# Two samples traced in the order of a table instead of turn by turn, in a four-layer attention kernel

## The chip, the core and the metric

The kernel runs on one core of one Trainium2 chip. The metric is device time of one execution in microseconds (us). TensorE is called PE here, VectorE DVE, ScalarE ACT, GpSimd POOL and SyncE SP, as in the profile.

## What is computed

The input is 16 samples of 256 channels by 32 x 32 positions, fp32. Four layers follow each other, each sample by itself:

```python
# layer 0 and layer 2 (own weights):
h = group_norm(x, 8 groups); q, k, v = linear(h)
x = x + proj(softmax(q.T @ k / 16) @ v)
# layer 1, a gate over positions:
m, M = mean(x, channels), max(x, channels)
x = x * sigmoid(conv3x3(m + M + relu(conv3x3([m, M]))))
# layer 3, q and k of 32 channels:
e = clip(q.T @ k / sqrt(32), -10, 10)
x = gamma * (softmax(e) @ v) + x
```

## The kernel before, in words

**Stages of a sample.** Layers 0 and 2 (`attend`) fold the query and key weights into one 256 x 256 matrix. First `seven` makes t = m x (banks tb, ta, tc, tf), then the values (`values`, banks vb, va, vc, vf). Then for each half h of the positions come two groups of logits (`logits`, banks sb, sa, sc, sf), their exponentials on ACT (L988, L990), and the product with the values (`weighted`, banks b, af, c). All these block products take seven block multiplications in place of eight, with sums and differences of blocks made on DVE. All go through one helper, so that their matmuls have one line, L877. A product's result is copied from its PSUM bank by ACT (L978 for logits, L1047 to L1063 in `weighted`) or added by DVE (L909, L1031). `weighted` makes combinations of the exponentials on DVE (L1004, L1005, L1050, L1056), and ends with the scaled residual (L1036).

**The gate.** `gate_of` makes two short matmul groups (c1 at L473, and c2). c1 reads row tiles that DVE and ACT shift by one position (`neighbours`, L458 and L459).

**Layer 3.** `clipped_attend` makes q and k with matmuls of 64 columns (`qk_products`, copied at L1394 and by ACT), values by `values`, and scores in sets. A set (`score_products`, L1401) is one h and one half mh of the keys: four tiles of 32 rows side by side on PE, each in a bank of its own, two matmuls a tile. ACT takes the exponentials from the four banks (`exponentials`, L1417), DVE clips them (`clip`, L1426), and `weighted` follows. A sample has four sets, 64 in all.

**Banks.** All products take banks from one PSUM pool of eight, in traced order: a new tile gets a bank that its previous tile's last reader has left.

**Lanes and turns.** Sample b runs on lane b % 2; even samples are `stream(0)`, odd ones `stream(1)`, both Python generators. A third, `later()`, holds the strips of layer 0's bias (L699), the head of sample 1, the weight transposes and folds of layers 2 and 3 (L623, L635), the gate's tables and checks of the weights. Each `yield` ends a turn; a turn issues a few products and what belongs to them. `wait(n)` spends n turns on nothing, for instance two between two score sets (`W_EXP`). The main loop (L1770 to L1776) gives `stream(0)` 30 turns ahead, each with one of `later`, and then goes turn by turn.

**Who orders what.** Only PE keeps the traced order. For DVE, ACT, POOL and SP, `Plan` makes the order after tracing: `durations` prices each step, `run` places step after step, `room` and `ready` tell when a step's tiles can have space, `needed` ranks steps by when PE wants them, and `pin` repeats that `ROUNDS` times, keeps the best and fixes each engine's order by dependences without a semaphore.

**Loads.** Inputs are issued on SP at the start (L554 x, L574 the layer-2 weights). The first tb_l waits for the normed x of sample 0 (L446).

Of the kernel before, what the change touches and what calls it, by code (L numbers as in the profile page):

```python
# [17 lines left out]
C = 256  # L18
# [20 lines left out]
L0_GAMMA, L0_BETA, L0_BQ, L0_BK, L0_BP = range(5)  # L39
L2_GAMMA, L2_BETA, L2_BQ, L2_BK, L2_BP = range(5, 10)  # L40
NVEC = 10
OFFSET = 30
ROUNDS = 3


W_PLANES, W_GATE1, W_GATE2, W_SEND1, W_NORM1, W_NORM2, W_NORM3, W_SEND2, W_EXP, W_AV, W_AV3 = 9, 2, 2, 4, 2, 10, 4, 7, 2, 2, 0
# [17 lines left out]
)  # L64
PE, DVE, ACT, POOL, SP = range(5)
SEEN = 44, 23, 23, 100, 60
RESTART, ENTRY, MARGIN = 102, 93, 1.04


class Book:  # L70
# [32 lines left out]
def elements(ap):  # L103
    return math.prod(n for _, n in ap[1:])


def durations(engine, ins, outs, reads, mode):


    ap = outs[0].ap  # L110
    n, parts = elements(ap), ap[0][1]
    if engine == PE:
        n = elements(reads[0].ap)
        if ins.is_transpose:
            return 110, 287
        if mode:
            return {"rows": (135, 496), "columns": (253, 403), "corner": (121, 210)}[mode]
        return max(224, 1.66 * n + 8), max(287, 0.84 * n + 178)
    if ins.opcode == "DMACopy":
        if "DRAM" in str(outs[0].tensor.space):  # L120
            return 480, 2500
        if n == 1024:
            return 480, 4600
        return 600, 5600 if n == 512 else 7200
    if engine == POOL:
        return 460 + 2 * n, 640 + 2 * n
    psum = any("PSUM" in str(a.tensor.space) for a in outs + reads)
    partial = 100 * (parts < P)
    if engine == ACT:
        issue = 50 + 0.83 * n if psum else 80 + 0.86 * n  # L130
        issue = MARGIN * max(210, issue + 100 * (len(reads) > 1) + partial)
        issue += 200 * (len(outs) - 1)
        return issue, issue + 180
    n = max([n] + [elements(a.ap) for a in reads])
    if ins.opcode not in ("TensorScalarPtr", "TensorCopy", "Reciprocal") or psum:
        issue = 60 + 1.045 * n
    elif sum(elements(a.ap) == n for a in reads) > 1:
        issue = 60 + 1.28 * n
    else:
        issue = 70 + 0.51 * n + 60 * max(0, len(reads) - 1)  # L140
    issue = MARGIN * max(90, issue + partial)
    return issue, issue + 157


class Plan:
# [79 lines left out]
    def run(self, rank):  # L225


        steps, n = self.steps, len(self.steps)
        begin, end = [0.0] * n, [None] * n
        free, mode = [0.0] * 5, ""  # L230
        live, next_of, placed = {}, dict.fromkeys(self.queues, 0), set()
        products = [i for i in range(n) if steps[i].engine == PE]
        at, missing = 0, [len(s.behind) for s in steps]
        waiting = [[i for i in range(n) if steps[i].engine == e and not missing[i]] for e in range(5)]
        order = [[] for _ in range(5)]

        def last_use(name):
            last = 0.0
            for j in self.users[name]:
                if end[j] is None:  # L240
                    return None
                last = max(last, end[j])
            return last

        def room(name):

            of, bufs = self.book.tiles[name]
            held = live.setdefault(of, [])
            if self.queues[of][next_of[of]] != name:
                return None  # L250
            if len(held) < bufs:
                return 0.0, None
            return min(
                ((t, o) for o in held for t in [last_use(o)] if t is not None), default=None
            )

        def ready(i):
            s = steps[i]
            t = 0.0
            for j in s.behind:  # L260
                if not steps[j].engine == s.engine == PE:
                    t = max(t, end[j])
            for name in s.tiles:
                if name not in placed:
                    r = room(name)
                    if r is None:
                        return None
                    t = max(t, r[0])
            return t and t + SEEN[s.engine]

        def place(i, t):
            nonlocal mode
            s = steps[i]
            for name in s.tiles:
                if name in placed:
                    continue
                placed.add(name)
                of, _ = self.book.tiles[name]
                old = room(name)[1]
                if old is not None:  # L280
                    live[of].remove(old)
                live[of].append(name)
                next_of[of] += 1
            more = 0
            if s.engine == PE:
                more = RESTART * (t > free[PE] > 0)
                if s.mode != mode:
                    t, more = (t + ENTRY, more) if s.mode else (t, RESTART)
                mode = s.mode
            begin[i], end[i] = t, t + s.done + more  # L290
            free[s.engine] = t + s.issue + more
            order[s.engine].append(i)
            for j in s.ahead:
                missing[j] -= 1
                if not missing[j] and steps[j].engine != PE:
                    waiting[steps[j].engine].append(j)

        for _ in range(n):
            best = None
            if at < len(products) and not missing[products[at]]:  # L300
                r = ready(products[at])
                if r is not None:
                    best = max(free[PE], r), products[at]
            for e in (DVE, ACT, POOL, SP):
                times = [(max(free[e], r), i) for i in waiting[e] for r in [ready(i)] if r is not None]
                if times:
                    t = min(times)[0]
                    i = min((rank[i], i) for u, i in times if u <= t + 1)[1]
                    if best is None or t < best[0]:
                        best = t, i  # L310
            t, i = best
            if steps[i].engine == PE:
                at += 1
            else:
                waiting[steps[i].engine].remove(i)
            place(i, t)
        return free[PE], order, begin
# [19 lines left out]
    def pin(self, tc):  # L337


        best, rank = None, [(0.0, i) for i in range(len(self.steps))]  # L340
        for _ in range(ROUNDS):
            found = self.run(rank)
# [167 lines left out]
def fast_path(nc, tc, k, bad, x, w_l0, w_l2, w_l3, qk_bias, v_bias, tap_idx, out):  # L510
# [7 lines left out]
    with ExitStack() as ctx:  # L518
# [328 lines left out]
        rows = [wts.tile([P, 3, STRIP], FP, name=f"rows{lane}") for lane in range(2)]  # L847
# [145 lines left out]
        def weighted(e, vt, tv, y, ri, h, nm):  # L993
# [30 lines left out]
            n0, n1 = h * TPH, h * TPH + 2  # L1024

            c1, c2 = slice(0, P), slice(P, C)
            lo, hi = slice(0, 2), slice(2, 4)
            acc = combp.tile([P, TPH, C + 1], FP, tag="acc", name=f"acc_{nm}_{h}")
# [29 lines left out]
            c = bank(f"c_{nm}_{h}")[:, : 2 * (P + 1)].rearrange("p (i c) -> p i c", i=2)  # L1058
            go(s1, t1, c, lone=False)
            nc.scalar.copy(acc[:, hi, P:], c)  # L1060
            yield
            go(s2, t2, b, fresh=False)
            nc.scalar.copy(acc[:, lo, c2], b)  # L1063
# [4 lines left out]
            for i in range(2):  # L1068
                done(i)
            yield  # L1070
            nc.vector.reciprocal(ri[:, n1 : n1 + 2], acc[:, hi, C])
            go(s3, t3, b, fresh=False)
            plus(hi, c2, b)
            plus(hi, c1, b)
# [644 lines left out]
        ready, tokens, late, running = {}, {}, [], [0]  # L1719
# [3 lines left out]
        def do_chores(lane, n=None):  # L1723
            for do in chores[lane][:n]:
                do()
            del chores[lane][:n]
# [3 lines left out]
        def in_turn(gens):  # L1730

            gens = list(gens)
            while gens:
                for g in list(gens):
                    if next(g, gens) is gens:
                        gens.remove(g)
                    else:
                        yield

        def later():  # L1740

            in_strips(bcol0, bstrip0, "l0")
            chores[0].extend(to_tokens(tokens[0]))
            yield from in_turn([head(1), fold("l2", 1, L2_GAMMA)])
            yield from fold3()
            chores[1].extend(to_tokens(tokens[1]))
            yield from k.build_toep(tc, work, tidx)
            yield from checks()

        def stream(first):  # L1750
            for b in range(first, B, 2):
                if b > 1:
                    chores[first].extend(to_tokens(tokens[b]))
                for _ in sample(b):
                    do_chores(first, 1)
                    yield
            do_chores(first)
            if first in running:
                running.remove(first)
# [7 lines left out]

        streams = [stream(0), stream(1)]  # L1770
        rest = later()
        for _ in range(OFFSET):
            next(streams[0])
            next(rest, None)
        for _ in in_turn([in_turn(streams), rest]):
            pass  # L1776


# [319 lines left out]
```

## Time and profile before

| what | us |
|---|---|
| median of 3 runs | 2646.5 (2644.03 to 2647.04) |
| the profiled execution, whole | 2642.92 |
| its span in the profile | 2641.1 |
| PE busy | 2622.2 |
| DVE busy | 2143.3 |
| ACT busy | 1349.1 |

The granted clock is 0.999 on average. An engine's busy time is the union of its instructions' time; the difference of the span to PE's busy time is not all of what PE waits, because a matmul's record also lasts through a short stall. For that the starts of single records are needed. In a timeline, the columns are start, duration, engine, line, operation, output and inputs with their sizes, number of records, and in brackets the idle time before and what ended it. A matmul on full fp32 data has two records.

### The profile page before, as it was taken

The numbers are of one execution on the slowest core, as the hardware profiler recorded it, in microseconds if no ns is written. First come the engines' busy times: TensorE is split into PE (matmuls) and PEld (weight loads), VectorE is DVE, ScalarE is ACT, GpSimd is POOL, SyncE is SP. The second block draws the span as 40 slices with busy tenths as digits, with TensorE's granted clock in tenths as the row PEclk, the third lists the DMA queues.
The fourth block names the chain that finished last, engine by engine and source line by source line (L and its number), as shares of the span: only waits on it lengthen the run. The fifth ranks groups of instructions, "written<-read, shape, count | busy, mean of one in ns | idle before, by whom it ended". The sixth has DMA issues, their size and how long they took to land.

```text
span 2641.1 us, 47888 instructions
## 1 busy us (share of the span) xinstructions
PE 2622.2 (99%) x18998; PEld 2368.0 (90%) x18998; DVE 2143.3 (81%) x4180; ACT 1349.1 (51%) x2825; POOL 69.7 (3%) x172
## 2 busy tenths in 40 slices
PE   8999999999999999999999999999999999999998
PEld 7888899888988989989889898998989989899897
DVE  8798887988778887788877888778887788878776
ACT  5454455544565445554555545555455544545453
POOL 5000000000000000000000000000000000000000
PEclk9999999999999999999999999999999999999999
DMA  4021211112121120211201212112111121101111
GB/s 118 1 65 49 57 33 37 53 49 65 25 57 49 41 73 9 57 56 41 65 17 49 65 33 65 32 34 65 49 49 33 33 65 49 49 17 33 49 39 44
DMA packets 135878, 123.08 MB, mean 47 GB/s; under 512 B 12768, under 2 KB 126688, under 8 KB 135648
## 3 DMA queue, kind: packets, MB, share of 16 engines
q1 hardware_dynamic: 133776, 118.76, 16.4%
q8 instruction: 153, 2.51, 0.4%
q10 hardware_dynamic: 1872, 1.18, 0.1%
q14 instruction: 77, 0.63, 0.1%
HBM read 69.58 MB, written 50.33 MB: 45 GB/s over the span
## 4 chain that ended last, share of the span: by engine, by line
PE 98%; DVE 1%; ACT 0%; DMA 0%; issue 0%; SPq 0%; DVEq 0%; ACTq 0%
PE b_l L877 19%; PE af_l L877 13%; PE c_l L877 13%; PE sb_l L877 13%; PE sc_l L877 8%; PE vb_l L877 5%; PE sf_l L877 4%; PE sa_l L877 4%; PE vc_l L877 3%; PE tb_l L877 3%; PE s L1401 3%; PE tc_l L877 2%; PE vf_l L877 2%; PE va_l L877 1%; PE tf_l L877 1%; PE qk L1375 1%
## 5 line engine op out<-in xcount | busy, mean ns | idle before, releaser
L877 PE MATMUL sb_l<-t_l,x 128*128 128x256 f32 x1024 | 256.9, 381 | 0.0
L877 PE MATMUL b_l<-vt,e_l 128*128 128x128 f32 x2048 | 250.2, 275 | 0.0
L877 PEld LDWEIGHTS b_l<-vt,e_l 128*128 128x128 f32 x2048 | 242.6, 192 | 4.9 <-issue 2.3
L988 ACT ACTIVATE e_l<-e_l 128x512 f32<-128x512 f32 x256 | 160.4, 630 | 119.0 <-DVE e_l L909 118.4
L877 PEld LDWEIGHTS sb_l<-t_l,x 128*128 128x128 f32 x1024 | 185.0, 190 | 31.8 <-issue 10.3
L978 ACT COPY e_l<-sb_l 128x512 f32<-128x512 f32 x256 | 149.1, 583 | 103.9 <-PE sb_l L877 102.3
L909 DVE TENSOR_TENSOR e_l<-sc_l,e_l 128x512 f32<-128x512 f32 x128 | 88.2, 689 | 119.2 <-PE sc_l L877 94.2
L877 PE MATMUL c_l<-tv,cb_l 128*128 128x129 f32 x1504 | 184.0, 275 | 0.0
L1417 ACT ACTIVATE e<-s 128x512 f32<-128x512 f32 x256 | 133.8, 601 | 97.0 <-PE s L1401 96.1
L909 DVE TENSOR_TENSOR e_l<-sb_l,e_l 128x512 f32<-128x512 f32 x256 | 172.9, 683 | 9.6 <-PE sb_l L877 5.0
L877 PEld LDWEIGHTS c_l<-tv,cb_l 128*128 128x128 f32 x1504 | 176.7, 191 | 0.8
L990 ACT ACTIVATE e_l<-e_l 128x1024 f32<-128x1024 f32 x128 | 135.2, 1056 | 76.2 <-DVE e_l L909 76.0
L793 ACT ACTIVATE xr<-xr,bstrip 128x128 f32<-128x128 f32 (+1 forms) x376 | 141.5, 437 | 16.2 <-DMA xr<-in_x_dram 10.2
L877 PE MATMUL sf_l<-tc_l,x 128*128 128x256 f32 x512 | 132.4, 381 | 0.0
L877 PE MATMUL sc_l<-tc_l,xs_l 128*128 128x256 f32 x512 | 131.6, 379 | 0.0
L877 PE MATMUL sa_l<-t_l,x 128*128 128x256 f32 x512 | 131.4, 379 | 0.0
L877 PE MATMUL sc_l<-t_l,xs_l 128*128 128x256 f32 x512 | 131.4, 379 | 0.0
L877 PE MATMUL sb_l<-tc_l,xs_l 128*128 128x256 f32 x512 | 131.4, 379 | 0.0
L877 PE MATMUL af_l<-vt,e_l 128*128 128x128 f32 x1024 | 127.2, 277 | 0.0
L877 PEld LDWEIGHTS af_l<-vt,e_l 128*128 128x128 f32 x1024 | 119.4, 192 | 8.1 <-issue 8.1
L877 PE MATMUL b_l<-tv,e_l 128*128 128x128 f32 x1024 | 125.7, 275 | 0.0
L877 PE MATMUL c_l<-vt,e_l 128*128 128x129 f32 x1024 | 125.4, 275 | 0.0
(304 smaller groups left out, 5840.6 us busy)
## 6 DMA issues: line engine op xcount, KB each, us to landing
x<-mid_x SPq DMA_DIRECT2D x64, 512.0 KB, 3.6
xr<-in_x_dram SPq DMA_DIRECT2D x64, 256.0 KB, 5.0
mid_x<-t_z SPq DMA_DIRECT2D x128, 128.0 KB, 2.3
mid_x<-t_l SPq DMA_DIRECT2D x128, 128.0 KB, 2.3
x<-in_x_dram SPq DMA_DIRECT2D x62, 256.0 KB, 3.8
out_dram<-xr SPq DMA_DIRECT2D x124, 128.0 KB, 2.3
raw_l<-in_w_l_dram SPq DMA_DIRECT2D x1, 1024.0 KB, 6.8
raw_l<-in_w_l_dram SPq DMA_DIRECT2D x2, 256.0 KB, 4.3
```

The lines of the kernel that those rows point to most:

```text
L793: nc.scalar.activation(y[:, s, ts], y[:, s, ts], AF.Identity, bias=bias[:, s : s + 1])
L877: mm = nc.tensor.matmul(out, left, right, start=fresh and m == 0 and (lone or i == 0), stop=(m == len(pairs) - 1), skip_group_check=True,)
L909: nc.vector.tensor_tensor(dst, src, dst, ALU.add)
L978: nc.scalar.copy(block(i, j), ps.rearrange("p (m n) -> p m n", m=2))
L988: nc.scalar.activation(part, part, AF.Exp)
L990: nc.scalar.activation(e[:, m : m + 2, :], e[:, m : m + 2, :], AF.Exp)
L1375: nc.tensor.matmul(ps[i * PH : (i + 1) * PH, : qt * P].rearrange("p (g n) -> p g n", g=qt), w3qk[:, c, i], xt[:, g0 : g0 + qt, c], start=( ...
L1401: nc.tensor.matmul(ss[g][:, j * 2 * P : (j + 1) * 2 * P].rearrange("p (t g j) -> p t g j", t=TPH, g=2), qk[gs, mh, 1 - blk, j * P : (j + 1 ...
L1417: nc.scalar.activation(by_strip[:, :, :, qa], ss[g].rearrange("p (m t n) -> p m t n", m=2, t=TPH), AF.Exp,)
```

## The change

Four parts. The numbers of lines in the new file are 36 higher from `weighted` on.

1. The tables FIRST_TURNS, TURNS (used CYCLES = 4 times) and LAST_TURNS name for each turn whose it is: 0 and 1 are the two streams, 2 is `later`. What the tables leave over goes turn by turn.
2. `ready` lets a tile be reserved only by its first traced use.
3. `Plan`'s constants change, among them the prices of the row and column tiles and of entering and leaving them, and a rule is added: an engine is held for a step of higher rank that becomes ready before the chosen one would end, and is needed within AHEAD.
4. In `weighted`, one reciprocal moves two turns ahead, directly behind ACT's copy that it reads.

```diff
-OFFSET = 30
-ROUNDS = 3
+FIRST_TURNS = (
+    "22222000000220000000000202000000020022022200200222002200010000221112100010100011"
...
+TURNS = (
+    "00000010111100111111100011001111111000110111111111011000100111000111111000111100"
...
+LAST_TURNS = (
+    "00000010111100111111100011001111111000110111111111011000100111000111111000111100"
...
+CYCLES = 4
+ROUNDS = 4
-RESTART, ENTRY, MARGIN = 102, 93, 1.04
+RESTART, ENTRY, EXIT, MARGIN = 102, 190, 205, 1.04
+AHEAD = 1000
-            return {"rows": (135, 496), "columns": (253, 403), "corner": (121, 210)}[mode]
+            return {"rows": (108, 496), "columns": (216, 403), "corner": (121, 210)}[mode]
-                    if r is None:
+                    if r is None or self.users[name][0] != i:
                         return None
-                    t, more = (t + ENTRY, more) if s.mode else (t, RESTART)
+                    t, more = (t + ENTRY, more) if s.mode else (t, EXIT)
                     i = min((rank[i], i) for u, i in times if u <= t + 1)[1]
+                    late = t + steps[i].issue
+                    soon = [
+                        (rank[j], u, j)
+                        for u, j in times
+                        if t + 1 < u < late and rank[j] < rank[i] and 1 < rank[j][0] < late + AHEAD
+                    ]
+                    if soon:
+                        _, t, i = min(soon)
             nc.scalar.copy(acc[:, hi, P:], c)
+            nc.vector.reciprocal(ri[:, n1 : n1 + 2], acc[:, hi, C])
             yield
...
-            nc.vector.reciprocal(ri[:, n1 : n1 + 2], acc[:, hi, C])
             go(s3, t3, b, fresh=False)
-        streams = [stream(0), stream(1)]
-        rest = later()
-        for _ in range(OFFSET):
-            next(streams[0])
-            next(rest, None)
-        for _ in in_turn([in_turn(streams), rest]):
+        streams = [stream(0), stream(1), later()]
+        for turn_of in FIRST_TURNS + CYCLES * TURNS + LAST_TURNS:
+            next(streams[int(turn_of)], None)
+        for _ in in_turn(streams):
             pass
```

More of the change, by code (lines that the diff above doesn't have):

```diff
@@ L41 @@
 NVEC = 10
-OFFSET = 30
-ROUNDS = 3
+FIRST_TURNS = (
+    "22222000000220000000000202000000020022022200200222002200010000221112100010100011"
+    "01121020220101002111112112200220011111221211111222201102220221012111100102121122"
+    "22000111102001000000001010000000010000010111101111111001000100100000000001000101"
+    "10011101001101111110011010111110111111100001010101110001111110101010000010000111"
+    "11111111000001000001000001110110110100000000000110110101001000101011111000000010"
+    "00101101011000010001000011111001111111000110011111111101111111110110001001110001"
+    "11111000111100001000011100000100000101101010111110001101000100000000001011100111"
+    "01011011111001001100101111101111111000100000110001101000010111000000111110011111"
+    "10111111000010010000111111100100110000110101100010111111000000001000001011001000"
+    "0110000101"
+)
+TURNS = (
+    "00000010111100111111100011001111111000110111111111011000100111000111111000111100"
+    "00100001110000010000010110101011111000110100010000000000101110011101011011111001"
+    "00110010111110111111100010000011000110100001011100000011111001111110111111000010"
+    "0100001111111001001100001101011000101111110000000010000010110010000110000101"
+)
+LAST_TURNS = (
+    "00000010111100111111100011001111111000110111111111011000100111000111111000111100"
+    "00100001110000010000010110101011111000110100010000000000101110011101011011111001"
+    "00110010111110111111100010000011000110100001011100000011111001111110111111000010"
+    "01000011111110010011000011010110010111110101000011110000001100001010000101111000"
+    "01111111000110011111000001100100100111100001111101101011111010111001111001000011"
+    "10000010000001000101000010000001011111000110100000111011001100010101101111100100"
+    "11001011111011111110001110111000011110000000011111000101101110111110100010010011"
+)
+CYCLES = 4
+ROUNDS = 4
 W_PLANES, W_GATE1, W_GATE2, W_SEND1, W_NORM1, W_NORM2, W_NORM3, W_SEND2, W_EXP, W_AV, W_AV3 = 9, 2, 2, 4, 2, 10, 4, 7, 2, 2, 0
```

## The prediction, as put on record

> **What bounds the kernel now.** I read the page first: the busy shares, then the chain that ended last.
>
> ```profile
> span 2641.1 us, 47888 instructions
> ...
> PE 2622.2 (99%) x18998; PEld 2368.0 (90%) x18998; DVE 2143.3 (81%) x4180; ACT 1349.1 (51%) x2825; POOL 69.7 (3%) x172
> ...
> PE 98%; DVE 1%; ACT 0%; DMA 0%; issue 0%; SPq 0%; DVEq 0%; ACTq 0%
> ```
>
> TensorE (PE) is busy 99% of the span and is 98% of the chain. So the time is PE's matmuls plus whatever gaps stand between them. The change orders the same matmuls differently (the built programs hold the same PE instructions), so only gaps can move. Next, the list of PE's waits:
>
> ```profile
> PE wtp_l L623 <- DMA raw_l<-in_w_l_dram: 4.8, 1, 4.8
> PE tb_l L877 <- DVE x L446: 2.0, 1, 2.0
> PE s L1401 <- DVE t_qk L1394: 1.7, 2, 0.9
> PE fold_l L635 <- DVE wt_l L629: 1.0, 1, 1.0
> ```
>
> About 10 us are named, all in the first 46 us or the last 50. The steady state hides its gaps in "busy", so I went to single records. Two back-to-back matmul records of 128 columns start 112 ns apart, of 256 columns 216 ns apart. Over a whole cycle (two samples, 324.3 us), only two kinds of place exceed that. The first is a score visit, that is, PE going into the 32-row tiles of layer 3 and back out. The timeline of PE shows it:
>
> ```profile
> 1012.65 1.03 PE L877 MATMUL sb_l<-t_l,x 128*128 128x256 f32 x4
> 1013.51 1.95 PE L877 MATMUL b_l<-vt,e 128*128 128x128 f32 x16
> 1015.39 1.15 PE L1401 MATMUL s<-t_qk 32*128 32x256 f32 x16
> 1016.47 2.05 PE L877 MATMUL b_l<-vt,e_l 128*128 128x128 f32 x16
> 1018.36 1.95 PE L877 MATMUL af_l<-tv,e_l 128*128 128x128 f32 x16
> ```
>
> Read start to start. Undisturbed, 16 records of a block product take 16 x 0.112 = 1.79. Here b_l lasts 1.88 before s and 1.89 after it, and s takes 1.08 where four rounds of four tiles side by side, at 0.216 a round, would be 0.865. The excess is 0.09 + 0.10 + 0.215 = 0.41 us a visit. The 64-column visits of q and k are untouched by the change.
>
> The second kind is the gate's first matmul (c1, L473) of the odd lane, which waits for ACT:
>
> ```profile
> 163.79 0.83 PE L877 MATMUL va_l<-wvp_l,x 128*128 128x128 f32 x6
> ...
> 164.38 0.24 ACT L459 COPY rows<-rows 32x62 f32<-32x62 f32 x1
> 164.67 0.52 PEld L473 LDWEIGHTS c_l<-rows,toep 128*128 128x128 f32 x4 [0.24 <-ACT rows L459]
> 164.67 0.63 PE L473 MATMUL c_l<-rows,toep 128*128 128x32 f32 x4
> ```
>
> ACT ends at 164.62, c1 starts at 164.67, 323 ns after the record before it instead of 112; the next record follows after 133 instead of 31. That is 0.31 us, the same in all eight cycles.
>
> **The change, part by part.**
>
> *Fewer score visits.* Comparing the built orders, before makes 64 score visits of one set; after makes 47: 30 of one set and 17 of two sets back to back. A second set appended costs its 4 x 0.216, and no entry or exit. Gain: 17 x 0.41 = 6.9 us. The Trainium skill (TensorEngine Tiling (Array Packing), Key Properties) says that changing the tiling mode drains the engine; that gives the sign, the row gives the price.
>
> *What the pairs cost.* The same page speaks against pairing: Gotcha 1, PSUM Pressure, says different row tiles write to different banks and software must synchronise them. Two sets take eight banks, all that the pool has. Taken at its harshest (the second set cannot start before the other users' banks are drained and the pair pays a full drain), the page would have the pair lose what it gained; so I walked it. In all 17 pairs but the last, the built order gives the fourth tile of the second set the bank of b_l of the sample's layer-3 (or of the other lane's layer-2) product, which closes just before the visit. It is freed by the two adds L1031 acc<-b. Taking DVE's prices from the rows below, for the odd-lane place (b, c, b of layer 3 after the last sb of layer 0; S is the end of sb):
>
> ```profile
> 1012.85 0.17 DVE L1066 RECIPROCAL ri<-c_l 128x2 f32<-128x2 f32 x1 [1.02 <-PE c_l L877]
> 1012.94 0.41 DVE L1031 TENSOR_TENSOR acc_l<-c_l,acc_l 128x256 f32<-128x256 f32 x1
> 1013.72 0.69 DVE L909 TENSOR_TENSOR e_l<-sb_l,e_l 128x512 f32<-128x512 f32 x1 [0.37 <-PE sb_l L877]
> ...
> 1015.32 1.21 DVE L1004 TENSOR_TENSOR cb_l<-e_l 128x1024 f32<-128x1024 f32 x1
> ```
>
> DVE starts 0.20 after the PE group that it waits for has given way (c_l to sb_l at 1012.65, reciprocal at 1012.85). So: first sb add S+0.21 to 0.90; ACT's exponential (L988, 0.63) to S+1.6; L1004 from S+1.65, L1005 from S+2.8, both 1.14 apart, free at S+3.95; reciprocal and acc<-c to S+4.35; two L1036 at 0.39 to S+5.15. b_l closes at S+3x1.79 = S+5.37, the adds run from S+5.57 to S+6.32 (0.34 spacing, 0.41 the second), seen by PE about 0.05 later (as c1 after ACT): S+6.37. The visit starts at S+5.37+0.09; the second set's fourth tile is due 0.32 + 3 x 0.216 + 0.02 after that: S+6.45. So it is just in time, by 0.08. In the even lane b_l follows sb directly, the adds have nothing ahead of them, and the margin comes out the same. Weights for a round are loaded one round ahead in the records (at S+6.23), so the load is late although the matmul need not be; c1 shows that an unhidden load costs about 0.1. Bounds: 0 (it hides) and 0.1 plus any DVE slip, say 0.3. I take 0.05, nearer to the walk: 17 x 0.05 = 0.8 us. Below nothing is excluded, since a wait is added and none taken away here.
>
> *Behind a pair* stand the first ACT exponential (L1417; starts 1.16 after the visit's start, as 1016.55 against 1015.39, 0.49 apart, 0.60 long) and the bank it frees: free at 1.8 from the visit's start, next full product due at 1.94. The copies L978 of the next logits stand after three exponentials in ACT's order, not after eight. DVE's clips (L1426) are due over 5 us later. I cost these at nothing; the cover is those 0.1 us and, further back, the logits or block products of the other lane.
>
> *c1 of the odd lane* now stands behind vb of layer 2, some 4.5 us of PE later; ACT's copy keeps its time. Gain 8 x 0.31 = 2.5 us. What reads c1 has 9.6 us of PE work as cover before c2 instead of 12.3, for a chain of 4 to 5 us.
>
> *Front.* The layer-2 weight transposes (L623) and the strips (L699) now stand ahead of the first tb_l (L877), which waited for DVE until 16.08. Their data is issued on SP at 10.08 and the page has that load landing after 6.8, so 16.9:
>
> ```profile
> 10.08 0.62 SPq L574 DMA_DIRECT2D raw_l<-in_w_l_dram  x1
> ```
>
> PE's idle of 2.0 (14.05 to 16.08) becomes 14.05 to 15.4 and 15.8 to 16.9, together 2.4: +0.4 us. The granted clock is 0.50 from 15.78 to 19.20 and 1.00 beside it. The Trainium skill (TensorE: Matmul & The Clock Gate, Part 1) ties half clock to an idle window of about 3.4 us; were another window lost by that rule, it would cost up to 1.7. Range -1 to +2.1; I take the idle sum. SP's and POOL's own orders do not change in the built programs.
>
> *No price:* the reciprocal two turns earlier (0.12 to 0.17 of DVE, not on the path), the planner's new constants and its rule of holding an engine (nothing on the chip), and runs of one lane's logits instead of alternating ones: such runs stand in before too, without a wait.
>
> **The sum.** 2642.9 (the profiled execution; span 2641.1 and 1.8 around it) - 6.9 - 2.5 + 0.8 + 0.4 = 2634.7, which is 8.2 less. Against the median of the runs, 2646.5, that is 2638.3. 0.2% (5.3 us) is about what a measurement of this kernel can tell from no change.
>
> **The rivals.**
> A (0.55): as summed, 2638.3; it runs from 2635.5 (pairs free, front gains 1) to 2641.
> B (0.20): the fourth bank is late by some tenths. For it: the margin is 0.08 and DVE is 81% busy. At 0.3 us a pair, 5.1 of the 9.0 net gain are lost: 2646.5 - 6.9 - 2.5 + 0.4 + 5.1 = 2642.6.
> C (0.14), slower: the full eight banks. After a pair the next logits need a bank from the exponentials, and their second product needs ACT's copy L978; if that copy waits behind all eight exponentials (1.16 + 8 x 0.49, then the copy's 0.58: 5.7 after the start, due at 4.5), each pair loses over 1.1 us. The break-even is 9.0/17 = 0.53 us a pair, slower by 0.2% from 0.84. At 1.0: 2646.5 - 9.0 + 17 = 2654.5. Against it: the copy stands after three exponentials.
> D (0.11): the gains come, but the new DVE and ACT orders put a wait of about 1 us into each cycle elsewhere: about 2646. For it: every product waits on one of those engines; against it: the covers that I found exceed 1 us.
>
> Faster: A and a little of B, 0.57. Within 0.2%: most of B and of D, 0.28. Slower: C and some of D, 0.15. The range runs from 2635 to 2648.5, leaving out most of C.
>
> **What would show it.** Right: 47 visits in the timeline, with score groups of 32 records of about 1.95 us; no c_l L473 wait on ACT in mid-run; PE busy less by about 9 us. B or C: a new line "s L1401 <- DVE acc" among PE's waits, or "sb_l <- ACT", and a two-set visit longer than 1.95. The front: first tb_l near 18 instead of 16.08. I am wrong if the 0.41 of a visit is not saved when two sets join, or if PE's sum falls and DVE's or ACT's idle before a product rises as much.

## The result and the profile after

The changed kernel takes 2637.66 us (median of 7 runs, 2635.85 to 2638.16) against 2645.96 for the kernel before (7 runs, 2642.59 to 2647.04): ratio 0.9969, 95% interval 0.9958 to 0.9981, so 8.3 us less. Measured once more on another occasion, the ratio was 0.9969 again (0.9958 to 0.998). The profiled executions differ by less: 2635.5 against 2641.1 of span, 5.6 us, and the same two kernels profiled a second time gave 2635.2 and 2641.1. I return to that difference below.

The page of the changed kernel, the same three rows:

```profile
span 2635.5 us, 48049 instructions
...
PE 2617.8 (99%) x18998; PEld 2374.0 (90%) x18998; DVE 2156.0 (82%) x4180; ACT 1348.8 (51%) x2825; POOL 74.2 (3%) x172
...
PE 98%; DMA 1%; ACT 0%; DVE 0%; SPq 0%; issue 0%; ACTq 0%
```

PE has as many instructions as before and is busy 4.4 us less, where the prediction's sign was about 9; it still is the chain. PE's waits:

```profile
PE wtp_l L659 <- DMA raw_l<-in_w_l_dram: 6.7, 2, 4.8
PE strips_l L735 <- DVE bcol L727: 2.0, 1, 2.0
PE b_end L913 <- ACT acc_end L1536: 0.5, 1, 0.5
...
PE s L1437 <- DVE t_qk L1430: 0.2, 1, 0.2
```

In the front, the wait of tb_l has become two, of strips_l and of the layer-2 transposes. In the tail, the score sets of the last sample wait 0.2 us for DVE where they waited 1.7.

The odd lane's pair in PE's timeline, at the place that the prediction walked:

```profile
1009.09 1.95 PE L913 MATMUL b_l<-tv,e 128*128 128x128 f32 x16
1010.87 1.95 PE L913 MATMUL c_l<-vt,e 128*128 128x129 f32 x16
1012.66 1.95 PE L913 MATMUL b_l<-vt,e 128*128 128x128 f32 x16
1014.54 2.10 PE L1437 MATMUL s<-t_qk 32*128 32x256 f32 x32
1016.57 2.05 PE L913 MATMUL b_l<-vt,e_l 128*128 128x128 f32 x16
```

One visit of 32 records, 2.03 from start to start. And DVE beside it:

```profile
1013.07 0.16 DVE L1103 RECIPROCAL ri<-c_l 128x2 f32<-128x2 f32 x1
1013.15 0.41 DVE L1067 TENSOR_TENSOR acc_l<-c_l,acc_l 128x256 f32<-128x256 f32 x1
1013.60 0.88 DVE L1072 SCALAR_TENSOR_TENSOR xr<-acc_l,ri,xr 128x256 f32<-128x256 f32 x2
1014.64 0.75 DVE L1067 TENSOR_TENSOR acc_l<-b_l,acc_l 128x256 f32<-128x256 f32 x2 [0.17 <-PE b_l L913]
```

With S = 1009.09, the adds that free the fourth bank run from S+5.55 to S+6.30; the walk had S+5.57 to S+6.32. From there the walk allowed 0.05 until PE sees the bank and so had it 0.08 early. In the record starts the fourth tile's weights are loaded at 1015.51 and its matmul starts at 1015.54, which is 0.15 after the last add ends at 1015.39: the bank is not early but late, by 20 ns. What that costs is seen in the distances of the 32 record starts, in ns (four tiles a round, from the visit's first record):

```
round 1 to 4:   7   7   6 300 |  7   7   6 196 |  7   6   7 196 |  7   6   7 196
round 5 to 8:   6   7  26 177 |  6   7 101 101 |  7   7 101 101 |  7   7 100 305
```

In round 5 the fourth tile starts 26 ns after the third instead of 6 or 7. From round 6 on it trails the other three by 0.10 us to the end. The rounds keep their 216 ns; the visit's exit is 0.095 later.

A ledger of PE's gaps, as the sum over all matmul starts of what exceeds the usual distance for that shape (visits included), with the second profile of each in brackets:

| part of the span | before | after | difference |
|---|---|---|---|
| to 60 us | 8.07 (8.70) | 8.71 (8.41) | +0.6 (-0.3) |
| 60 to 2560 us | 26.72 (26.74) | 22.81 (22.86) | -3.9 (-3.9) |
| after 2560 us | 6.83 (6.74) | 4.74 (4.74) | -2.1 (-2.0) |

Two visits that before makes after 2560 us (at 2565 and 2570) are one pair at 2557.8 after the change. So of the 17 visits fewer, 15 are missing from the middle row and two from the last.

### The profile page after: what moved, and what is told of

It reads as the page before. It is cut to its first block, busy times and chain, and to the rows that moved or that the text cites. A ratio compares the mean times of both kernels' runs of the same rounds, so it can differ in the third digit from the quotient of the medians.

```text
span 2635.5 us, 48049 instructions
## 1 busy us (share of the span) xinstructions
PE 2617.8 (99%) x18998; PEld 2374.0 (90%) x18998; DVE 2156.0 (82%) x4180; ACT 1348.8 (51%) x2825; POOL 74.2 (3%) x172
## 4 chain that ended last, share of the span: by engine, by line
PE 98%; DMA 1%; ACT 0%; DVE 0%; SPq 0%; issue 0%; ACTq 0%
PE b_l L913 19%; PE af_l L913 13%; PE c_l L913 13%; PE sb_l L913 13%; PE sc_l L913 8%; PE vb_l L913 5%; PE sf_l L913 4%; PE sa_l L913 4%; PE vc_l L913 3%; PE tb_l L913 3%; PE s L1437 3%; PE tc_l L913 2%; PE vf_l L913 2%; PE va_l L913 2%; PE qk L1411 1%; PE ta_l L913 1%
## 5 line engine op out<-in xcount | busy, mean ns | idle before, releaser
L1096 ACT COPY acc_l<-c_l 128x258 f32<-128x258 f32 x94 | 35.3, 376 | 197.7 <-PE c_l L913 197.5
L913 PE MATMUL af_l<-tv,e_l 128*128 128x128 f32 x1024 | 125.5, 275 | 0.0
```

The costliest lines, as they stand in the source:

```text
L913: mm = nc.tensor.matmul(out, left, right, start=fresh and m == 0 and (lone or i == 0), stop=(m == len(pairs) - 1), skip_group_check=True,)
```

## The experiments

Medians are given with the ratio to the kernel before on the same occasion. "Mid-run" is the middle row of the ledger. In the tables, a digit is a turn; the edits are shown for one cycle and hold for every like place.

**Pairs split.** Theory: the visits saved time. Rival: the rest of the new order did.

```diff
 TURNS, even lane's pair (two sets, then the other lane):
-00001
+00100
 odd lane's pair:
-1110
+1101
```

> The changed kernel, but in all 17 pairs the second score set stands one turn of the other lane later, so that PE makes 64 score visits again; front, gate and planner stay as changed. Theory (a joined pair saves an entry and exit of 0.41 us, less 0.10 for a late fourth bank): 17 x 0.31 = 5 us more than the changed kernel, about 2643, and every visit lasts 1.08 us. Rival (the visits are not what saved time; the rest of the new order is): within 1.5 us of the changed kernel's 2637.7.

Measured: 2641.3 us, ratio 0.9979 (0.9969 to 0.9988). PE makes 64 visits, mid-run gaps are 27.03 against 22.81: 4.2 us more. That is what the terms give: 16 of the 17 new visits lie in mid-run, 16 x 0.41 = 6.6, less the 2.4 that the pairs' waits had cost (below). The rival falls by the trace: with the visits back, the mid-run gaps are those of before. The runs alone would not decide it, since the interval overlaps with that of the changed kernel (0.9958 to 0.9981). This profile's span is only 2636.0, because its front had the smallest gaps of all (see the clock below).

**The tables with the old planner, and the old turns with the new one.** Which half of the change brings it?

```diff
 (a) tables kept
-RESTART, ENTRY, EXIT, MARGIN = 102, 190, 205, 1.04
-AHEAD = 1000
+RESTART, ENTRY, MARGIN = 102, 93, 1.04
-ROUNDS = 4
+ROUNDS = 3
 and the old prices, without "soon" and without the first-use rule
 (b) new planner kept
-        for turn_of in FIRST_TURNS + CYCLES * TURNS + LAST_TURNS:
-            next(streams[int(turn_of)], None)
-        for _ in in_turn(streams):
+        for _ in range(OFFSET):
+            next(streams[0])
+            next(rest, None)
+        for _ in in_turn([in_turn(streams), rest]):
```

> The tables and the earlier reciprocal, with the planner of before (old constants, old rule for reserving a tile, no holding of an engine, 3 rounds). Theory (PE's order alone brings the gain): within 2 us of the changed kernel's 2637.7, with 47 visits. Rival (the planner's new prices and rules are needed, because the joined pairs have no slack for a wrong order on DVE and ACT): pairs longer than 2.1 us, time back at 2643 or above.

> The old turn-by-turn order with the new planner and the earlier reciprocal. Theory (PE's order brings the gain): 64 visits, c1 of the odd lane still waits, 2646 +- 2. Rival (the planner's part is worth some us by itself): below 2643.

Measured: (a) 2640.61, ratio 0.9975 (0.9964 to 0.9986), which is 1.6 us over the changed kernel by the ratios; 47 visits, mid-run 21.25, even 1.6 under the changed kernel, pairs of 2.04 us; tail 7.96. The rival for (a) falls. (b) 2642.09, ratio 0.9983 (0.9974 to 0.9992); mid-run 26.61, all eight waits of c1 there, tail 6.74. So the mid-run gain is the tables' alone. The tail's is neither's alone: in (a) its wait is the old one,

```profile
PE s L1428 <- DVE t_qk L1421: 1.7, 2, 0.9
```

and in (b) it is 1.6; only both together bring it to 0.2. For (b) the runs and the profile disagree: the runs are 4.5 us faster than before, as the rival had it, while the profile shows 0.2 us of difference to before in mid-run and tail together, as the theory had it. That gain lies in no gap of a kept trace.

It goes with the granted clock, whose mean the results hold for every run. Of the 55 runs of the kernel before that were made beside these experiments, 19 have 0.999 and a median of 2644.06; 24 have 0.996 or 0.997 and a median of 2647.46. Both kept traces of before have 0.999. Over all kernels here, 35 of 79 runs with the old planner are below 0.998, five of (a)'s seven among them, and 3 of 67 with the new one: one of (b)'s 11 (2646.78, its slowest), none of the changed kernel's 15. The one kept trace with 0.997 is that of (a). PE's clock, third from the end in the row, is at half there in the tail too, from 2594.66 to 2598.07:

```profile
2590.00:2600.00 10.00, 8.29 (x64) 7.11 (x67) 6.61 (x12) 7.63 (x18) 0.00 (x0) 0.83 0.20 52
```

That stretch costs 1.4 us of (a)'s 7.96. The lists show that clock, time and planner go together, not what causes what; where in the span the runs of before with the lower clock lose their time, no kept trace shows.

**The gate later, in the kernel before.** To get c1's term alone, c1 was moved one turn, then c1 and c2 together:

```diff
-W_PLANES, W_GATE1, W_GATE2 = 9, 2, 2
+W_PLANES, W_GATE1, W_GATE2 = 10, 1, 2    (c1 alone)
+W_PLANES, W_GATE1, W_GATE2 = 10, 2, 1    (c1 and c2)
```

> The kernel before, with the gate's first matmul one turn later in both lanes (one turn more ahead of it, one fewer behind it, so that c2 keeps its place). Theory (the 0.31 us wait of the odd lane's c1, eight times): 2.5 us less than before, about 2643.5, and no wait of c1 on ACT in the trace. Rival (the wait only moves to what follows, c2 or the next layer's normalisation): within 0.5 us of before.

> The kernel before with both short groups of the gate, c1 and c2, one turn later in both lanes, and the last wait of the gate one turn shorter. In the run that moved c1 alone the wait of c1 went and c2 waited 0.19 us in its place, so that nothing was gained. Theory (c1's 0.31 us is a gain where c2 keeps its distance from c1): neither c1 nor c2 waits in mid-run, 2.5 us less of PE gaps there than before. Rival (what reads the gate then comes late, the normalisation and layer 2): a new wait at tb_l or at the score sets.

Measured: c1 alone 2646.15, ratio 0.9996 (0.9987 to 1.0005). c1's wait is gone, but c2 (L490) now stands still 0.19 beyond its usual distance eight times, where c1 had 0.21 (0.29 and 0.31 with the record behind it): the rival was right. Both: 2655.96, ratio 1.0039 (1.0026 to 1.0053), slower. The rival again, and dearer:

```profile
1134.17 1.95 PE L877 MATMUL b_l<-vt,e_l 128*128 128x128 f32 x16
1137.40 1.10 PE L877 MATMUL tb_l<-x,m_l 128*128 128x512 f32 x2 [1.28 <-issue]
```

Layer 2's tb_l needs what follows the gate, and waits 1.45 us more than usual in each of eight places. So in the turn-by-turn order the 0.31 could not be had by moving the gate. That the changed kernel gets it is read from its own trace (no c1 wait but one of 0.25 at the last, and no new one at c2 or tb_l); it is not shown by an isolated run.

**One single set later.** The changed kernel's trace had a wait that nobody had forecast, the odd lane's second set of half 0:

```profile
986.14 1.15 PE L1437 MATMUL s<-t_qk 32*128 32x256 f32 x16
987.21 1.16 PE L913 MATMUL vb_l<-wvp_l,x 128*128 128x128 f32 x8
988.30 1.52 PE L1437 MATMUL s<-t_qk 32*128 32x256 f32 x16
989.75 1.13 PE L913 MATMUL sb_l<-t_l,x 128*128 128x256 f32 x4
```

The second s takes 1.45 from start to start, not 1.08, in six cycles. By the built order its third tile takes the bank of vc_l, which this add frees:

```profile
987.35 0.68 DVE L901 TENSOR_TENSOR tv<-vt,tv 128x512 f32<-128x512 f32 x1
987.95 0.68 DVE L945 TENSOR_TENSOR vt<-vc_l,vt 128x512 f32<-128x512 f32 x1
```

PE was done with vc_l at 986.1, but DVE makes value sums of the other lane first. Edit:

```diff
-110
+101
```

> The changed kernel, with the odd lane's second score set of half 0 (a single set that in the changed kernel's trace lasts 1.45 us instead of 1.08) one turn of the other lane later, behind the first logits of layer 0. Theory (its third tile's bank waits for DVE's value add, which stands behind three value sums): the wait goes in six cycles, 2.2 us less than the changed kernel, about 2635.5. Rival (DVE is simply behind there, and the next product then waits as long): within 0.5 us of the changed kernel.

Measured: 2635.26, ratio 0.9964 (0.995 to 0.9978). All single visits in mid-run last 1.08, and the gaps there are 20.63: 2.2 less, as expected to the tenth. The theory holds by the trace; the runs alone do not tell this kernel from the changed one.

**Pairs later.** Is the 0.1 of a pair the late bank?

```diff
 even lane's pair:
-00001
+10000
 odd lane's pair:
-1110
+0111
```

> The changed kernel, with all 17 pairs one turn of the other lane later, so that the adds that free the fourth bank are done long before. Theory (a pair lasts 2.035 us instead of 1.94 because that bank comes just in time): pairs of 1.94 us, 17 x 0.095 = 1.6 us and up to 0.8 more at two late pairs, so about 2635.5 to 2636. Rival (two sets back to back always cost the 0.1): pairs stay at 2.03 and the time at 2637.7 or above.

> Both moves together. Theory: the gains add, 3.8 to 4.6 us less than the changed kernel, about 2633.5. Rival: what is moved later runs into the next waits, no better than the better of the two.

Measured: 2652.81, ratio 1.0031 (1.0019 to 1.0043), and with the single set moved too 2651.42, ratio 1.0024 (1.0015 to 1.0033): slower than before. I had overlooked that one turn later the other lane's new products hold banks. Now only the first set's exponentials can free the last ones:

```profile
1019.55 1.95 PE L913 MATMUL b_l<-vt,e_l 128*128 128x128 f32 x16
1021.43 1.57 PE L1437 MATMUL s<-t_qk 32*128 32x256 f32 x22
1023.25 1.13 PE L1437 MATMUL s<-t_qk 32*128 32x256 f32 x10 [0.26 <-ACT e L1453]
```

A pair lasts 2.89 (odd) or 3.13 (even) instead of 2.04. This is a shortage of banks like the prediction's rival C, though at the second set itself and not at the logits behind the pair: 0.85 to 1.09 a pair. Neither of my two expectations for this run was right, and both moves together, where the gains should have added, failed with it. That the 0.1 is a late bank therefore rests on the record starts of the changed kernel (only the fourth tile shifts, and its weights are loaded 0.12 after the add that frees its bank), not on this run; that two sets back to back cost it in any case is not excluded by a run.

**The front.**

```diff
-FIRST_TURNS: 2222200000022000
+FIRST_TURNS: 0202020202020200
```

> The changed kernel with the first 16 turns as before: layer 0 of sample 0 alternates with the strips and the layer-2 weight transposes instead of waiting behind them. Theory (the front of the changed kernel costs 0.6 us by its trace: two idles of 1.9 us and a half clock up to 21 us): 0.6 to 2 us less, about 2636.5. Rival (the loads and the clock set that time, whatever the order): within 0.4 us.

> The changed kernel with the odd lane's single score set one turn later and the first 16 turns as before. Theory: the mid-run gain of the first (2.2 us) is kept; the front depends on how many half-clock windows fall into it (none, one or two in the profiles so far, each some 1.7 us), more than on the order: 2633.5 to 2636.

> The changed kernel once more, unchanged, for the spread of its front. Theory (the mid-run is fixed, the front is not): PE's gaps from 60 to 2560 us within 0.2 us of the first profile, the front different by up to 3.5 us with the number of half-clock windows; ratio to before 0.9969 +- 0.001.

> The kernel before once more, unchanged. Theory: PE's gaps from 60 to 2560 us within 0.2 us of the first profile, the front by up to 3.5 us different; the profile of before that the prediction was made from had one half-clock window and a whole time 3 us under its median, so a profile nearer to the median should have a costlier front.

Measured: the first 2636.0, ratio 0.9966 (0.9952 to 0.9979), not told apart from the changed kernel's 0.9969. With the single set moved too, 2633.84, ratio 0.9956 (0.9942 to 0.9969): the lowest median here, but its lead over either change alone (0.9964 and 0.9966) is within the intervals. What goes with the front's gaps is the granted clock. The windows view, with the clock third from the end of each row, for the changed kernel:

```profile
12.40:15.80 3.40, 1.53 (x12) 1.37 (x10) 3.21 (x15) 0.75 (x3) 2.41 (x5) 0.94 0.88 284
15.80:19.20 3.40, 1.44 (x12) 1.35 (x13) 0.98 (x4) 1.45 (x2) 0.00 (x0) 0.50 0.60 192
19.20:22.60 3.40, 3.40 (x10) 2.07 (x9) 3.40 (x10) 0.54 (x1) 3.19 (x6) 0.56 0.73 149
```

and for the kernel with split pairs, whose first turns are the same:

```profile
12.40:15.80 3.40, 2.90 (x20) 2.58 (x20) 3.32 (x16) 1.68 (x5) 1.69 (x4) 1.00 1.02 367
15.80:19.20 3.40, 3.23 (x21) 2.12 (x22) 3.26 (x10) 1.79 (x3) 2.72 (x7) 1.00 0.49 135
```

No half clock there, 3.4 us of it in the profile of before, 6.8 in that of the changed kernel, 3.4 in its second profile. But the view shows 1.00 for all the time ahead of the first recorded change of the clock. The matmuls show that PE starts at half rate in every profile: eight records of 256 columns take 3.58 us from start to start in the kernel with split pairs, 0.45 each, where 0.216 is usual, and 2.70 in the changed kernel, where the recorded change comes at 8.56 and not at 11.39:

```profile
7.04 3.78 PE L671 MATMUL fold_l<-wt_l 128*128 128x256 f32 x8
10.62 1.32 PE L696 MATMUL tbp_l<-vec,wt_l 128*128 128x1 f32 x8
```

```profile
6.76 2.87 PE L671 MATMUL fold_l<-wt_l 128*128 128x256 f32 x8
9.46 0.95 PE L696 MATMUL tbp_l<-vec,wt_l 128*128 128x1 f32 x8
```

With that start counted, the six profiles that have these first turns and the new planner rank alike by the time at half rate (6.3, 8.9, 9.5, 9.7, 10.6 and 12.2 us) and by the front's gaps (5.1, 7.3, 8.3, 8.4, 8.7 and 9.3 us). Both second profiles came out as expected in mid-run, within 0.05 us of the first. What I expected of the second profile of before, a whole time nearer to its median, did not come: 2642.91 after 2642.92.

## Why the prediction was right, and where its terms were not

The forecast was 2638.3, the measured median 2637.66; the mechanism was case A. Against the profile, the terms:

| step | predicted, us | in the traces, us |
|---|---|---|
| visits, 64 to 47 | -6.9 | -6.9: 47 visits, entry +0.09, exit +0.10, as before |
| c1 of the odd lane | -2.5 | -2.3: gone seven times, 0.25 left at the last |
| pairs, late fourth bank | +0.8 | +2.4: 15 x 0.095 = 1.4, and two pairs with +0.30 and +0.63 |
| a wait of the new DVE order in each cycle | 0 (case D: 1 us a cycle) | +2.2: 6 x 0.37, the single set |
| front | +0.4 | +0.6, and -0.3 in the second profiles |
| tail, beside two of the 17 visits | 0 | -1.5: by the record starts the last sample's first set waits 1.7 less, the rest is 0.2 more |

These add to -5.5 with the first front; PE's last matmul starts 5.35 earlier. The other 0.15 is in gaps too small to assign.

*Visits.* Right in number and size; the split pairs confirm them.

*Pairs.* The mechanism was right and the adds fell within 20 ns of the walk; the size was off. The step that failed is the 0.05 from the add to PE: it was taken from c1, and the fourth tile took 0.15, so that a margin of 0.08 became a lateness of 0.02. The term "I take 0.05" measured 0.095: of the two bounds, an unhidden weight load, 0.1, was the right end, and the records keep that distance to the end of the visit. The two pairs in other surroundings (the first odd one at 385 us and the last one) were not walked, only assumed to be like the rest.

*No price.* Here the prediction failed in a part: "the planner's new constants and its rule of holding an engine (nothing on the chip)". They do order DVE: with the old planner the single set does not wait, and with the new one it does, 2.2 us in all; and only with the new one, together with the tables, does the tail's wait fall from 1.7 to 0.2. Two errors of opposite sign, +2.2 and -1.5, hid each other. The walk covered the pairs and skipped the single sets, on the ground that covers there exceeded 1 us.

*Front.* The range -1 to +2.1 held, but +0.6 beside +0.4 is luck. The two idles took 3.8 us where the walk had 2.4, the first tb_l starts at 20.11 where it was due near 18, and a second half-clock stretch came. Against that stands a wait of 1.0 (fold_l for DVE's wt_l) that is gone, which the walk did not look at. A front read from one profile is one draw of several.

*The sum against the median.* The runs moved 8.3, the profiled spans 5.6 to 5.9. The profile of before is 3 us under its median, twice; that of the changed kernel is at its median, twice. The run of the old turns with the new planner shows the same without the tables: 0.2 in the profile, 4.5 to 4.9 in the runs. So some 2.6 us of what was measured is in no term of the prediction. It goes with the granted clock, and that with the planner: 24 of 55 runs of before have a mean clock under 0.998, none of 15 after. Why stays open. The forecast's hit to 0.6 us is therefore in part luck: by the terms that it named, it should have been some 2.5 us too low.

## What to carry to other kernels

When PE is 99% busy, look at the starts of single matmul records: a tiling mode that is entered and left 64 times cost 26 us inside "busy". Join such visits where both lanes have just closed their products, and count banks: one turn later the same join cost more than it saved. If a scheduler orders the other engines, give its new order a price, walking every place where a bank is handed over, not only those that the change names.

## What the runs showed of the hardware

- A tile whose bank comes 20 ns late in round 5 of 8 stays 0.10 us behind the other three of its visit, without slowing the rounds (216 ns), and passes 0.095 us on at the exit.
- PE starts at half rate in every profile (matmuls of 128 columns 0.213 us apart instead of 0.112), for 3.8 to 6.3 us. After that, executions with the same first turns have no, one or two stretches of 3.4 us at 0.50 in the first 24 us, and 5.1 to 9.3 us of gaps with it. From 60 to 2560 us two profiles of one kernel agree within 0.05 us.
- The mean granted clock of a run of before lies between 0.996 and 0.999, and its time moves with it: the median is 2647.7 us at 0.996 and 2644.1 at 0.999.
